# Last two blocks of a cross-attention kernel: seven-product queries and projections, and division behind the values

## Chip, cores and metric

One Trainium2 chip, one core. The metric is the device time of the whole kernel in microseconds, median of several runs. One further execution was profiled; its page, waits and timeline are what is read here.

## What is computed

x is 16 x 1024 x 512, the context 16 x 64 x 512, all float32. Both are layer-normalised with a scale and shift that depend on the condition, then 16 heads of width 32 attend from 1024 rows to 64 context rows.

```python
xq  = _ada_ln(x_q,  t_vec, Wss_q,  bss_q)
xkv = _ada_ln(x_kv, t_vec, Wss_kv, bss_kv)
q = (xq @ Wq + bq).reshape(B, Lq, nh, dh)
kv = (xkv @ Wkv + bkv).reshape(B, Lkv, 2, nh, dh)
k, v = kv[:, :, 0], kv[:, :, 1]
scores = jnp.einsum('bqhd,bkhd->bhqk', q, k) / jnp.sqrt(jnp.float32(dh))
attn = jax.nn.softmax(scores, axis=-1)
out = jnp.einsum('bhqk,bkhd->bqhd', attn, v).reshape(B, Lq, H)
return x_q + (out @ Wp + bp)
```

## The kernel before

The 16 x 1024 rows are cut into 32 blocks (0 to 31) of 512 rows; two blocks share a batch entry and its keys and values. The schedule is written out by hand: the calls stand in program order, every engine takes its own instructions in that order, and each waits only for the data and buffers that it needs. There is a way in (blocks 0 to 3), a loop over i = 4 to 29 (L1139 to L1233), and a way out (L1237 to L1293) in which y = 30 and z = 31. In the code below, `y - 1` is block 29 and `y - 2` block 28.

What happens to a block, and on which engine (PE is TensorE, DVE VectorE, ACT ScalarE, POOL GpSimd, SP the queue that issues DMAs):

- its rows are loaded, normalised (ACT), turned by DVE in squares of 32 and moved by 16 DMAs into a feature-major tile `xt`; `scale_features` (L562) applies scale and shift;
- queries: PE multiplies by Wq, a copy with bias goes to `qt`;
- `scores` (L666), in two halves z of the 64 context rows: PE fills two PSUM tiles of the pool `ps_s`; DVE reduces maxima out of each (L685) while ACT copies the scores to SBUF (L694). With `crossed` the two engines begin on different tiles;
- `maxima` (L721): the two halves' maxima are joined and spread out over a full tile (L716, 2.3 us on DVE); `subtract` (L727, two instructions), `weights` (L733, exponentials on ACT, two instructions);
- the sum of the weights, the product with the values (`mix`, L809, PE), division by the sum, projection by Wp, addition of x, and the write to DRAM.

Two forms exist for three of these steps.

**Queries.** The plain form (`queries`, L533) uses 16 matmuls of 512 columns. The form of the loop (`query_product`, L607) divides matrix and block into 2 x 2 parts and forms seven products instead of eight (four matmuls of 256 columns each), from sums of parts made beforehand on POOL (`query_weight_sums` once, `feature_sums` for each block, four instructions). The seven share two PSUM banks, `qa[0]` and `qa[1]`; `query_seed` copies one bank to the other, and four parts leave them by `query_out` (ACT, two instructions each) and `query_added` (DVE).

**Projection.** The plain form (`project` and `projected`, L849 to L868) makes four tiles of 128 rows, each in a bank of its own from a ring of four; one DVE addition to the residual and one write of 256 KB follow each. There the bias is added to the residual beforehand (`residual`, L330, on POOL). The form of the loop (`product`, `added`, L915 to L953) again has seven products, numbered 1 to 7, in two banks: `acc[2]` takes 1, 6, 5, 3 in that order, `acc[3]` takes 2, and, after a fresh filling, 7 and 4. `biased` (L891, ACT) fills a bank with the bias ahead of 1 and 7; `added` (DVE, L947) adds what the bank holds at that moment to a quarter of the residual, after every product. So a product that goes on in a bank has to wait until the addition of the one before has read it. `row_sums` (L903, POOL, two calls of two instructions) makes the sums of parts, partly in place.

**Division.** In the plain form DVE sums both halves of the weights (`sums`), inverts and spreads the result (`inverse`), and `divide` multiplies both weight tiles by it before `mix`. In the form of the loop POOL adds the two weight tiles (`total`, L765), DVE reduces the sum (`row_total`) and inverts it (`inverse_rows`), five DMAs take the small result to DRAM and back in another order, `spread_rows` (L792, DVE) spreads it, and `divided` (L800) multiplies the mixed values by it as they leave PSUM.

In the loop the two forms' waits are spread out: between `product(b, 6)` and `product(b, 5)` stand a query product of another block and half of the scores; between `product(a, 2)` and `product(a, 7)` stand four query products. The way out of the kernel before ends the loop form with block 28; blocks 29 to 31 take the plain projection, block 31 the plain queries, blocks 30 and 31 the plain division (block 29's is done behind the values). Block 31's scores use the buffers `big2` and `big3`, those of block 29. `load_residual` (L144) of block 30 takes the buffer of block 28's residual, so it waits for that block's last write; SP takes its DMAs in order behind it.

Of the kernel before, what the change touches and what calls it, by code (L numbers as in the profile page):

```python
# [9 lines left out]
F32 = mybir.dt.float32  # L10
# [10 lines left out]
def cross_attention_block(  # L21
# [88 lines left out]
    def bank(name, k=None):  # L110
        if k is None:
            k = ring.pop(0)
            ring.append(k)
        return ps_m.tile([P, TB], F32, tag=f"mm{k}", name=name)
# [215 lines left out]
    def residual(i, ts=range(NT)):  # L330
        for t in ts:
            nc.gpsimd.tensor_add(r_tiles[i][:, t, :], r_tiles[i][:, t, :], b_p_sb)
# [260 lines left out]
    def feature_sums(i):  # L593

        if "xt" not in sums_of:
            sums_of["xt"] = qpool.tile([P, 4, 2, HC, P], F32, tag="wq", name="xt_sums")
        t = sums_of["xt"]
        tt = nc.gpsimd.tensor_tensor
        b12 = feature_half(i, 0, 1)
        tt(t[:, 0], feature_half(i, 1, 1), b12, ALU.subtract)  # L600
        tt(b12, b12, feature_half(i, 0, 0), ALU.subtract)
        tt(t[:, 1], feature_half(i, 1, 1), b12, ALU.subtract)
        tt(t[:, 2], feature_half(i, 1, 0), t[:, 1], ALU.subtract)
# [62 lines left out]
    def scores(i, z, crossed=False):  # L666

        kt, qt = k_tiles[i // BPB], qt_tiles[i]
        pss = [ps_s.tile([P, 2, TB], F32, tag="s", name=f"ps_{i}_{z}_{e}") for e in range(2)]
        for r in range(HPC):  # L670
            rows = slice(32 * r, 32 * r + 32)
            for c in range(NC):
                nc.tensor.matmul(  # L673
                    pss[r // 2][32 * c : 32 * c + 32, r % 2, :],
                    lhsT=kt[rows, c, z * HK : (z + 1) * HK],
                    rhs=qt[rows, c, :],
                    start=True,
                    stop=True,
                )
        if z == 0:  # L680
            m_tiles[i] = small.tile([P, 2, HPC, NJ], F32, tag="m2", name=f"m2_{i}")
        s_sb = big.tile([P, HPC, TB], F32, tag=f"big{i % 2 * 2 + z}", name=f"s_{i}_{z}")

        def maximum(e):
            nc.vector.tensor_reduce(  # L685
                m_tiles[i][:, z, 2 * e : 2 * e + 2, :],
                pss[e].rearrange("p r (j a) -> p r j a", a=32),
                AX.X,
                ALU.max,
                apply_transpose=True,  # L690
            )

        def copied(e):
            nc.scalar.copy(s_sb[:, 2 * e : 2 * e + 2, :], pss[e])  # L694


        for step in (
            ((maximum, 0), (copied, 1), (maximum, 1), (copied, 0))
            if crossed
            else ((maximum, 0), (copied, 0), (maximum, 1), (copied, 1))  # L700
        ):
            step[0](step[1])
        s_tiles[i, z] = s_sb

    def both(dst, src, op):

        nc.vector.tensor_reduce(dst, src.rearrange("p z r j -> p (r j) z"), AX.X, op)

    def spread(i, src, name, other=False):
        if other:  # L710

            t = qpool.tile([P, 4, NC, NT * 32], F32, tag="xt", name=name)
            t = t.rearrange("p g c n -> p (g c n)")
        else:
            t = rpool.tile([P, HPC * TB], F32, tag="spread", name=name)
        nc.vector.transpose(t, src.unsqueeze(2).to_broadcast([P, HPC * NJ, 32]))  # L716
        return t.rearrange("p (r q) -> p r q", r=HPC)
# [3 lines left out]
    def maxima(i):  # L721

        m = small.tile([P, HPC * NJ], F32, tag="m", name=f"m_{i}")
        both(m, m_tiles.pop(i), ALU.max)
        mb_tiles[i] = spread(i, m, f"mb_{i}", other=i == NB - 1)

    def subtract(i, eng=nc.gpsimd, zs=(0, 1)):  # L727
        for z in zs:
            eng.tensor_tensor(s_tiles[i, z], s_tiles[i, z], mb_tiles[i], ALU.subtract)  # L729
# [3 lines left out]
    def weights(i, z):  # L733
        p = s_tiles[i, z]
        nc.scalar.activation(p, p, AF.Exp, scale=SCALE)  # L735
# [14 lines left out]
    def inverse(i):  # L750

        v = small.tile([P, HPC * NJ], F32, tag="v", name=f"v_{i}")
        both(v, l_tiles.pop(i), ALU.add)
        nc.vector.reciprocal(v, v)
        vb_tiles[i] = spread(i, v, f"vb_{i}", other=i in (1, NB - 1))

    def divide(i, eng=nc.gpsimd):
        vb = vb_tiles.pop(i)
        for z in range(2):
            eng.tensor_tensor(s_tiles[i, z], s_tiles[i, z], vb, ALU.mult)  # L760
# [3 lines left out]

    def total(i):  # L765

        t = big.tile([P, HPC, TB], F32, tag=f"big{(i + 1) % 2 * 2}", name=f"sum_{i}")
        nc.gpsimd.tensor_tensor(t, s_tiles[i, 0], s_tiles[i, 1], ALU.add)  # L768
        sum_tiles[i] = t

    def row_total(i):
        lt_tiles[i] = small.tile([P, HPC, NJ], F32, tag="lt", name=f"lt_{i}")
        nc.vector.tensor_reduce(
            lt_tiles[i],
            sum_tiles.pop(i).rearrange("p r (j a) -> p r j a", a=32),
            AX.X,
            ALU.add,
            apply_transpose=True,
        )

    def inverse_rows(i):

# [16 lines left out]

    def divided(i):  # L800
        vb = vb_tiles.pop(i)
        ot_tiles[i] = opool.tile([P, NC, TB], F32, tag="ot", name=f"ot_{i}")
        for e in range(2):
            cs = slice(2 * e, 2 * e + 2)
            nc.vector.tensor_tensor(ot_tiles[i][:, cs, :], po_tiles[i][e], vb[:, cs, :], ALU.mult)

    po_tiles, ot_tiles = {}, {}

    def mix(i, apart=True):  # L809

        vt = v_tiles[i // BPB]

        if apart:
            pairs = [ps_s.tile([P, 2, TB], F32, tag="s", name=f"po_{i}_{e}") for e in range(2)]
            po = [pairs[c // 2][:, c % 2, :] for c in range(NC)]
            po_tiles[i] = pairs
        else:
            po = [bank(f"po_{i}_{c}") for c in range(NC)]
            po_tiles[i] = po
        for z in range(2):  # L820
            p = s_tiles.pop((i, z))
            for c in range(NC):
                rows = slice(32 * c, 32 * c + 32)
                for r in range(HPC):
                    nc.tensor.matmul(  # L825
                        po[c][32 * r : 32 * r + 32, :],
                        lhsT=vt[rows, z, 32 * r : 32 * r + 32],
                        rhs=p[rows, r, :],
                        start=(z == 0),
                        stop=(z == 1),  # L830
                    )
# [110 lines left out]
    def added(i, n):  # L942

        m, o = {1: (0, 0), 2: (0, 0), 6: (0, 1), 7: (1, 1), 5: (1, 1), 4: (0, 1), 3: (1, 0)}[n]
        r = r_tiles[i][:, 2 * m : 2 * m + 2, o * HO : (o + 1) * HO]
        k = 2 if n in (1, 6, 5, 3) else 3
        nc.vector.tensor_add(r, acc[k].rearrange("p (t h) -> p t h", t=2), r)  # L947
        if n in (3, 4):
            nc.sync.dma_start(
                rows_of(out, i)[:, 2 * m : 2 * m + 2, :], r_tiles[i][:, 2 * m : 2 * m + 2, :]  # L950
            )
        if n == 3:
            r_tiles.pop(i)  # L953


    q_stats(0)
# [182 lines left out]
    for i in range(4, NB - 2):  # L1139
# [78 lines left out]
            q_stats(i + 4, (3,), kvb=kvb if kv == 0 else None)  # L1218
        query_product(n, 3)
        query_out(n, 3)  # L1220
        if f < NB - 1:
            feature_sums(f)
        else:
            residual(i)
        product(a, 7)
        row_total(i)
        inverse_rows(i)
# [7 lines left out]


    y, z = NB - 2, NB - 1  # L1237
    residual(z)
    scores(y, 0, crossed=True)
    product(y - 2, 6)  # L1240
    added(y - 2, 6)
    added(y - 2, 7)
    scores(y, 1)
    product(y - 2, 5)
    added(y - 2, 5)
    maxima(y)
    subtract(y, nc.vector)
    queries(z, 0)
    product(y - 2, 4)
    product(y - 2, 3)  # L1250
    spread_rows(y - 1)
    added(y - 2, 4)
    added(y - 2, 3)
    ring[:] = [1, 2, 3, 0]
    load_residual(y)
    mix(y - 1)
    divided(y - 1)
    weights(y, 0)
    queries(z, 1)
    sums(y, 0)  # L1260
    weights(y, 1)
    residual(y)
    queries(z, 2)
    sums(y, 1)
    queries(z, 3)
    inverse(y)
    divide(y)
    scores(z, 0)
    project(y - 1, 0)
    scores(z, 1)  # L1270
    maxima(z)
    project(y - 1, 1)
    subtract(z, nc.vector)
    project(y - 1, 2, later=True)
    mix(y)
    weights(z, 0)
    mixed(y, (0,))
    weights(z, 1)
    mixed(y, (1,))
    sums(z, 0)  # L1280
    projected(y - 1, 2)
    sums(z, 1)
    inverse(z)
    divide(z, nc.vector)
    project(y - 1, 3)
    project(y, 0)
    project(y, 1)
    project(y, 2)
    mix(z)
    mixed(z)  # L1290
    project(y, 3)
    for t in range(NT):
        project(z, t)  # L1293

# [1 line left out]
_INS = [  # L1296
# [37 lines left out]
```

## Time and profile before

| what | value |
|---|---|
| median of 3 runs | 1058.74 us |
| lowest, highest | 1057.19, 1059.29 us |
| profiled execution, time | 1058.86 us |
| profiled execution, span | 1057.1 us |
| busy in the span: PE | 1033.6 us (98%) |
| DVE, POOL, ACT | 854.7 (81%), 752.7 (71%), 618.0 us (58%) |
| one repetition of the loop (945.84 to 975.10) | 29.26 us |
| way out (975.10 to the end) | 82.0 us |

Times in the profile count from the start of the span; the execution's own time is 1.76 us longer than its span. A row of a timeline gives start, duration, engine, line, operation, what is written from what, and how many instructions were merged; in brackets stands how long the engine was idle before it and what ended that. PE's rows overlap slightly, since matmuls are pipelined.

### The profile page before, as it was taken

To read this page: it belongs to the slowest core of one execution; us is meant where nothing else is said; L and a number is where in the kernel's file an instruction comes from. 1 tells how busy PE (TensorE), PEld (TensorE's weight loads), DVE (VectorE), ACT (ScalarE), POOL (GpSimd) and SP (SyncE) were. 2 spreads that over 40 slices of the span, in tenths; PEclk is the share of its full clock that TensorE was granted. 3 is DMA by queue.
4 is the path that set the end of the run, shared out by engine and by line. 5 is a ranking of instruction groups with operands and counts; after the bars stand their busy time and mean duration, and the time that the engine had idled before them with its cause. 6 is when DMAs were issued, how large, how long until landed. Compare 5 with 4: busy or idle time off the path is not lost.

```text
span 1057.1 us, 22537 instructions
## 1 busy us (share of the span) xinstructions
PE 1033.6 (98%) x8914; PEld 733.7 (69%) x8914; DVE 854.7 (81%) x1134; ACT 618.0 (58%) x951; POOL 752.7 (71%) x470
## 2 busy tenths in 40 slices
PE   6999998999999999999999999999999999999998
PEld 4534365777777787777787787777777777777433
DVE  5698648987789877888878878898778887776993
ACT  3566665665575655667556666566566765565330
POOL 0258794889768869788668986688886886787340
PEclk9999999999999999999999999999999999999999
DMA  9743444444535344544345443444454443334202
GB/s 337 248 127 111 130 122 127 155 150 147 161 94 162 123 140 145 171 148 127 106 131 164 153 158 112 126 141 150 139 157 134 152 134 116 98 115 162 82 30 90
DMA packets 99976, 147.27 MB, mean 139 GB/s; under 512 B 29944, under 2 KB 30096, under 8 KB 99872
## 3 DMA queue, kind: packets, MB, share of 16 engines
q1 hardware_dynamic: 99872, 145.85, 43.5%
q8 instruction: 70, 1.15, 0.5%
q14 instruction: 34, 0.28, 0.1%
HBM read 78.85 MB, written 34.44 MB: 107 GB/s over the span
## 4 chain that ended last, share of the span: by engine, by line
PE 80%; DVE 5%; POOL 5%; DMA 4%; SPq 2%; issue 2%; ACT 1%; POOLq 0%; DVEq 0%; ACTq 0%
PE pp L933 28%; PE pq L625 27%; PE po L825 6%; PE ps L673 6%; PE pp L852 5%; PE pq L542 3%; SPq L508 2%; PE pv L431 2%; PE pk L395 2%; POOL s L760 2%; DMA wss_kv<-in_L_xcond_Wss_kv_dram 2%; DMA b_p_sb<-in_L_xcond_bp_dram 1%; POOL s L729 1%; DMA x<-in_x_dram 1%; DVE s L729 1%
## 5 line engine op out<-in xcount | busy, mean ns | idle before, releaser
L729 POOL TENSOR_TENSOR s<-s,mb 128x2048 f32<-128x2048 f32 x58 | 263.1, 4560 | 160.8 <-DVE mb L716 160.8
L694 ACT COPY s<-ps 128x1024 f32<-128x1024 f32 x128 | 129.5, 1012 | 119.7 <-DVE m L685 82.9
L685 DVE TRANSPOSE_TENSOR_REDUCE m<-ps 128x32 f32<-128x1024 f32 x128 | 150.6, 1214 | 27.1 <-PE ps L673 27.1
L655 ACT ACTIVATE qt<-pq,bias_t 128x256 f32<-128x256 f32 x208 | 85.8, 463 | 110.9 <-PE pq L625 110.9
L933 PE MATMUL pp<-w_p_sb,ot 128*128 128x256 f32 x648 | 148.7, 379 | 0.0
L735 ACT ACTIVATE s<-s 128x2048 f32<-128x2048 f32 x64 | 122.3, 1911 | 42.4 <-POOL s L729 31.8
L947 DVE TENSOR_TENSOR r<-pp,r 128x512 f32<-128x512 f32 x189 | 122.5, 670 | 25.5 <-PE pp L933 19.8
L933 PEld LDWEIGHTS pp<-w_p_sb,ot 128*128 128x128 f32 x648 | 123.4, 190 | 17.4 <-issue 0.7
L768 POOL TENSOR_TENSOR sum<-s,s 128x2048 f32<-128x2048 f32 x27 | 122.7, 4543 | 0.8 <-ACT s L735 0.8
L933 PEld LDWEIGHTS pp<-WT,s 128*128 128x128 f32 x432 | 78.9, 192 | 54.0 <-issue 29.3
L933 PE MATMUL pp<-WT,s 128*128 128x256 f32 x432 | 109.3, 397 | 0.0
L933 PE MATMUL pp<-WT,ot 128*128 128x256 f32 x432 | 102.2, 380 | 0.0
L625 PE MATMUL pq<-xt_sums,wq_sums 128*128 128x256 f32 x416 | 101.0, 386 | 0.0
L321 ACT ACTIVATE x<-x,rstdq 128x512 f32<-128x512 f32 x128 | 96.7, 807 | 4.8 <-POOL rstdq L285 3.2
L625 PE MATMUL pq<-xt,wq_sums 128*128 128x256 f32 x416 | 99.0, 381 | 0.0
L625 PEld LDWEIGHTS pq<-xt_sums,wq_sums 128*128 128x128 f32 x416 | 77.0, 190 | 31.1 <-issue 21.8
L625 PE MATMUL pq<-xt,w_q_sb 128*128 128x256 f32 x416 | 98.4, 380 | 0.1
L260 DVE BATCH_NORM_STATS2 bs<-x 128x6 f32<-128x512 f32 x128 | 86.9, 679 | 5.0 <-DMA x<-in_x_dram 5.0
L662 DVE TENSOR_TENSOR qt<-pq,qt 128x256 f32<-128x256 f32 x104 | 39.1, 418 | 63.1 <-PE pq L625 62.5
L933 PEld LDWEIGHTS pp<-WT,ot 128*128 128x128 f32 x432 | 82.2, 190 | 11.0
L565 ACT ACTIVATE xt<-xt,ss_q 128x512 f32<-128x512 f32 x112 | 84.7, 810 | 6.1 <-DMA xt<-ht 4.3
L625 PEld LDWEIGHTS pq<-xt,w_q_sb 128*128 128x128 f32 x416 | 79.1, 190 | 11.0 <-PE pp L933 0.4
(139 smaller groups left out, 1725.0 us busy)
## 6 DMA issues: line engine op xcount, KB each, us to landing
x<-in_x_dram SPq DMA_DIRECT2D x32, 1024.0 KB, 6.4
r<-in_x_dram SPq DMA_DIRECT2D x32, 1024.0 KB, 5.5
xt<-ht SPq DMA_DIRECT2D x496, 64.0 KB, 2.0
out_dram<-r SPq DMA_DIRECT2D x54, 512.0 KB, 3.8
out_dram<-r SPq DMA_DIRECT2D x20, 256.0 KB, 2.0
wss_q<-in_L_xcond_Wss_q_dram SPq DMA_DIRECT2D x2, 1024.0 KB, 8.8
ctx<-in_ctx_dram SPq DMA_DIRECT2D x8, 256.0 KB, 3.2
wss_kv<-in_L_xcond_Wss_kv_dram SPq DMA_DIRECT2D x2, 1024.0 KB
```

The lines of the kernel that those rows point to most:

```text
L260: nc.vector.bn_stats(bs, r)
L321: nc.scalar.activation(dst, src, AF.Identity, bias=rstd[:, 1, j : j + 1], scale=rstd[:, 0, j : j + 1])
L565: nc.scalar.activation(xt[:, :, c, :], xt[:, :, c, :], AF.Identity, scale=ss["q"][:, c, b : b + 1], bias=ss["q"][:, NC + c, b : b + 1],)
L625: nc.tensor.matmul(qa[k][:, m * HT : (m + 1) * HT].rearrange("p (g n) -> p g n", g=2), lhsT=a[:, c, m * P : (m + 1) * P], rhs=x[:, :, c, : ...
L655: nc.scalar.activation(dst, src, AF.Identity, bias=bq_t[:, o : o + 1])
L685: nc.vector.tensor_reduce(m_tiles[i][:, z, 2 * e : 2 * e + 2, :], pss[e].rearrange("p r (j a) -> p r j a", a=32), AX.X, ALU.max, apply_tra ...
L694: nc.scalar.copy(s_sb[:, 2 * e : 2 * e + 2, :], pss[e])
L729: eng.tensor_tensor(s_tiles[i, z], s_tiles[i, z], mb_tiles[i], ALU.subtract)
L735: nc.scalar.activation(p, p, AF.Exp, scale=SCALE)
L768: nc.gpsimd.tensor_tensor(t, s_tiles[i, 0], s_tiles[i, 1], ALU.add)
L933: nc.tensor.matmul(acc[k][:, t * HO : (t + 1) * HO], lhsT=rows[:, c, t * P : (t + 1) * P], rhs=cols[:, c, :], start=n == 2 and t == 0 and ...
L947: nc.vector.tensor_add(r, acc[k].rearrange("p (t h) -> p t h", t=2), r)
```

## The change

It keeps the loop but for its last repetition and rewrites the way out. Helpers get the variants that this needs: block 31's scores lie in `ht` and `xt`, block 30's total in `x`, block 30's divided values in `big2`, so that each has a place of its own; `mix` can be given its four banks; `divided` then goes bank by bank and fills `acc[2]` after the first; `halves_total` joins the two sums of block 31; the last block's `added` writes each finished quarter at once, the last one in two parts.

```diff
@@ -679,7 +679,12 @@
                 )
         if z == 0:
             m_tiles[i] = small.tile([P, 2, HPC, NJ], F32, tag="m2", name=f"m2_{i}")
-        s_sb = big.tile([P, HPC, TB], F32, tag=f"big{i % 2 * 2 + z}", name=f"s_{i}_{z}")
+        if i < NB - 1:
+            pool, tag = big, f"big{i % 2 * 2 + z}"
+        else:
+
+            pool, tag = ((hpool, "ht"), (qpool, "xt"))[z]
+        s_sb = pool.tile([P, HPC, TB], F32, tag=tag, name=f"s_{i}_{z}")
 
         def maximum(e):
             nc.vector.tensor_reduce(
@@ -722,7 +727,7 @@
 
         m = small.tile([P, HPC * NJ], F32, tag="m", name=f"m_{i}")
         both(m, m_tiles.pop(i), ALU.max)
-        mb_tiles[i] = spread(i, m, f"mb_{i}", other=i == NB - 1)
+        mb_tiles[i] = spread(i, m, f"mb_{i}", other=False)
 
     def subtract(i, eng=nc.gpsimd, zs=(0, 1)):
         for z in zs:
@@ -752,7 +757,7 @@
         v = small.tile([P, HPC * NJ], F32, tag="v", name=f"v_{i}")
         both(v, l_tiles.pop(i), ALU.add)
         nc.vector.reciprocal(v, v)
-        vb_tiles[i] = spread(i, v, f"vb_{i}", other=i in (1, NB - 1))
+        vb_tiles[i] = spread(i, v, f"vb_{i}", other=i == 1)
 
     def divide(i, eng=nc.gpsimd):
         vb = vb_tiles.pop(i)
@@ -764,7 +769,8 @@
 
     def total(i):
 
-        t = big.tile([P, HPC, TB], F32, tag=f"big{(i + 1) % 2 * 2}", name=f"sum_{i}")
+        pool, tag = (xpool, "x") if i == NB - 2 else (big, f"big{(i + 1) % 2 * 2}")
+        t = pool.tile([P, HPC, TB], F32, tag=tag, name=f"sum_{i}")
         nc.gpsimd.tensor_tensor(t, s_tiles[i, 0], s_tiles[i, 1], ALU.add)
         sum_tiles[i] = t
 
@@ -778,6 +784,10 @@
             apply_transpose=True,
         )
 
+    def halves_total(i):
+        lt_tiles[i] = small.tile([P, HPC, NJ], F32, tag="lt", name=f"lt_{i}")
+        both(lt_tiles[i].rearrange("p r j -> p (r j)"), l_tiles.pop(i), ALU.add)
+
     def inverse_rows(i):
 
         lt = lt_tiles.pop(i)
@@ -799,14 +809,22 @@
 
     def divided(i):
         vb = vb_tiles.pop(i)
-        ot_tiles[i] = opool.tile([P, NC, TB], F32, tag="ot", name=f"ot_{i}")
-        for e in range(2):
-            cs = slice(2 * e, 2 * e + 2)
-            nc.vector.tensor_tensor(ot_tiles[i][:, cs, :], po_tiles[i][e], vb[:, cs, :], ALU.mult)
+        pool, tag = (big, "big2") if i == NB - 2 else (opool, "ot")
+        ot = pool.tile([P, NC, TB], F32, tag=tag, name=f"ot_{i}")
+        ot_tiles[i] = ot
+        po = po_tiles.pop(i)
+        for e in range(len(po)):
+            if len(po) == NC:
+                nc.vector.tensor_tensor(ot[:, e, :], po[e], vb[:, e, :], ALU.mult)
+                if e == 0:
+                    biased(i, 2)
+            else:
+                cs = slice(2 * e, 2 * e + 2)
+                nc.vector.tensor_tensor(ot[:, cs, :], po[e], vb[:, cs, :], ALU.mult)
 
     po_tiles, ot_tiles = {}, {}
 
-    def mix(i, apart=True):
+    def mix(i, apart=True, ks=(None,) * NC):
 
         vt = v_tiles[i // BPB]
 
@@ -815,7 +833,7 @@
             po = [pairs[c // 2][:, c % 2, :] for c in range(NC)]
             po_tiles[i] = pairs
         else:
-            po = [bank(f"po_{i}_{c}") for c in range(NC)]
+            po = [bank(f"po_{i}_{c}", ks[c]) for c in range(NC)]
             po_tiles[i] = po
         for z in range(2):
             p = s_tiles.pop((i, z))
@@ -944,13 +962,21 @@
         m, o = {1: (0, 0), 2: (0, 0), 6: (0, 1), 7: (1, 1), 5: (1, 1), 4: (0, 1), 3: (1, 0)}[n]
         r = r_tiles[i][:, 2 * m : 2 * m + 2, o * HO : (o + 1) * HO]
         k = 2 if n in (1, 6, 5, 3) else 3
-        nc.vector.tensor_add(r, acc[k].rearrange("p (t h) -> p t h", t=2), r)
+        a = acc[k].rearrange("p (t h) -> p t h", t=2)
+        if i == NB - 1:
+
+            for ts in ((0,), (1,)) if n == 3 else ((0, 1),):
+                ts = slice(ts[0], ts[-1] + 1)
+                nc.vector.tensor_add(r[:, ts, :], a[:, ts, :], r[:, ts, :])
+                if n in (2, 3, 4, 5):
+                    dst = rows_of(out, i)[:, 2 * m : 2 * m + 2, o * HO : (o + 1) * HO]
+                    nc.sync.dma_start(dst[:, ts, :], r[:, ts, :])
+            return
+        nc.vector.tensor_add(r, a, r)
         if n in (3, 4):
             nc.sync.dma_start(
                 rows_of(out, i)[:, 2 * m : 2 * m + 2, :], r_tiles[i][:, 2 * m : 2 * m + 2, :]
             )
-        if n == 3:
-            r_tiles.pop(i)
 
 
     q_stats(0)
@@ -1218,10 +1244,7 @@
             q_stats(i + 4, (3,), kvb=kvb if kv == 0 else None)
         query_product(n, 3)
         query_out(n, 3)
-        if f < NB - 1:
-            feature_sums(f)
-        else:
-            residual(i)
+        feature_sums(f)
         product(a, 7)
         row_total(i)
         inverse_rows(i)
@@ -1235,62 +1258,112 @@
 
 
     y, z = NB - 2, NB - 1
-    residual(z)
     scores(y, 0, crossed=True)
     product(y - 2, 6)
     added(y - 2, 6)
+    query_product(z, 1)
+    query_seed(z)
     added(y - 2, 7)
     scores(y, 1)
     product(y - 2, 5)
     added(y - 2, 5)
     maxima(y)
-    subtract(y, nc.vector)
-    queries(z, 0)
+    subtract(y)
+    query_product(z, 2)
+    query_out(z, 2)
     product(y - 2, 4)
-    product(y - 2, 3)
     spread_rows(y - 1)
     added(y - 2, 4)
+    query_product(z, 6)
+    query_out(z, 6)
+    query_product(z, 7)
+    query_out(z, 7)
+    weights(y, 0)
+    query_product(z, 5)
+    query_added(z, 5)
+    query_product(z, 4)
+    query_added(z, 4)
+    query_product(z, 3)
+    query_out(z, 3)
+    weights(y, 1)
+    total(y)
+    product(y - 2, 3)
     added(y - 2, 3)
-    ring[:] = [1, 2, 3, 0]
     load_residual(y)
-    mix(y - 1)
+    scores(z, 0, crossed=True)
+    mix(y - 1, apart=False, ks=(2, 3, 1, 0))
     divided(y - 1)
-    weights(y, 0)
-    queries(z, 1)
-    sums(y, 0)
-    weights(y, 1)
-    residual(y)
-    queries(z, 2)
-    sums(y, 1)
-    queries(z, 3)
-    inverse(y)
-    divide(y)
-    scores(z, 0)
-    project(y - 1, 0)
+    row_sums(y - 1, 0)
+    row_total(y)
+    inverse_rows(y)
+    product(y - 1, 1)
+    added(y - 1, 1)
     scores(z, 1)
+    product(y - 1, 2)
+    added(y - 1, 2)
+    biased(y - 1, 3)
+    row_sums(y - 1, 1)
     maxima(z)
-    project(y - 1, 1)
-    subtract(z, nc.vector)
-    project(y - 1, 2, later=True)
+    product(y - 1, 7)
+    added(y - 1, 7)
+    subtract(z, nc.vector, (0,))
+    subtract(z, nc.gpsimd, (1,))
+    product(y - 1, 6)
+    added(y - 1, 6)
+    product(y - 1, 5)
+    added(y - 1, 5)
+    product(y - 1, 3)
+    added(y - 1, 3)
+    biased(y, 2)
+    weights(z, 0)
     mix(y)
-    weights(z, 0)
-    mixed(y, (0,))
+    spread_rows(y)
+    product(y - 1, 4)
+    divided(y)
+    row_sums(y, 0)
+    added(y - 1, 4)
     weights(z, 1)
-    mixed(y, (1,))
     sums(z, 0)
-    projected(y - 1, 2)
+    product(y, 1)
+    added(y, 1)
+    product(y, 2)
+    added(y, 2)
+    biased(y, 3)
+    row_sums(y, 1)
     sums(z, 1)
-    inverse(z)
-    divide(z, nc.vector)
-    project(y - 1, 3)
-    project(y, 0)
-    project(y, 1)
-    project(y, 2)
+    halves_total(z)
+    inverse_rows(z)
+    product(y, 7)
+    added(y, 7)
+    product(y, 6)
+    added(y, 6)
+    product(y, 5)
+    added(y, 5)
+    product(y, 3)
+    added(y, 3)
+    biased(z, 2)
     mix(z)
-    mixed(z)
-    project(y, 3)
-    for t in range(NT):
-        project(z, t)
+    spread_rows(z)
+    product(y, 4)
+    divided(z)
+    row_sums(z, 0)
+    added(y, 4)
+    product(z, 1)
+    added(z, 1)
+    product(z, 2)
+    added(z, 2)
+    biased(z, 3)
+    row_sums(z, 1)
+    product(z, 7)
+    added(z, 7)
+    product(z, 6)
+    added(z, 6)
+    product(z, 5)
+    added(z, 5)
+    product(z, 4)
+    added(z, 4)
+    product(z, 3)
+    added(z, 3)
```

## The prediction

> **What bounds the kernel now.** I compared the last repetition of the loop with the way out by stages, then read TensorE's timeline of the way out, then those of the engines that its new waits would be for. First the stages; after the stage come each engine's busy time and count, then TensorE's clock.
>
> ```profile
> 945.84:975.10 29.26, 29.26 (x242) 22.42 (x241) 20.48 (x23) 15.49 (x21) 23.73 (x12) 1.00 0.46 147
> 975.10:1005.00 29.90, 29.40 (x229) 14.52 (x229) 29.62 (x25) 10.71 (x11) 12.70 (x11) 1.00 0.21 73
> 1005.00:1035.00 30.00, 28.17 (x198) 10.84 (x211) 28.23 (x19) 9.37 (x8) 12.07 (x5) 1.00 0.07 27
> 1035.00:1057.10 22.10, 18.32 (x72) 7.58 (x44) 5.06 (x8) 1.93 (x2) 0.00 (x0) 0.97 0.28 107
> ```
>
> In the loop TensorE (PE) never rests and VectorE (DVE) has 30% free. In the way out PE still hardly rests, but DVE is as full: 29.6 of 29.9 us and 28.2 of 30.0. So there are two near bounds there, and it matters who waits for whom. PE's own rows, from the timeline:
>
> ```profile
> 971.55 1.89 PE L625 MATMUL pq<-xt,wq_sums 128*128 128x256 f32 x8
> 973.28 1.89 PE L933 MATMUL pp<-WT,ot 128*128 128x256 f32 x8
> 975.10 1.14 PE L673 MATMUL ps<-qt,kt 32*32 32x512 f32 x32
> 976.17 2.00 PE L933 MATMUL pp<-WT,s 128*128 128x256 f32 x8
> ...
> 1003.32 3.70 PE L852 MATMUL pp<-w_p_sb,ot 128*128 128x512 f32 x8
> 1006.95 1.14 PE L673 MATMUL ps<-qt,kt 32*32 32x512 f32 x32
> ...
> 1033.61 2.35 PE L825 MATMUL po<-s,vt 32*32 32x512 f32 x64
> 1035.88 17.43 PE L852 MATMUL pp<-w_p_sb,ot 128*128 128x512 f32 x40
> ```
>
> Rows overlap by the pipeline's tail, so I take start to start: one of the seven products 1.73 us (971.55 to 973.28), a half of the scores 1.07, the values 2.28, a whole projection tile 3.44. The way out starts at 975.10 with block 30's scores; PE ends at about 1053.3.
>
> The rows that follow PE, and the one wait that I expect to be new:
>
> ```profile
> L685 DVE TRANSPOSE_TENSOR_REDUCE m<-ps 128x32 f32<-128x1024 f32 x128 | 150.6, 1214 | 27.1 <-PE ps L673 27.1
> L947 DVE TENSOR_TENSOR r<-pp,r 128x512 f32<-128x512 f32 x189 | 122.5, 670 | 25.5 <-PE pp L933 19.8
> ...
> 968.31 0.83 ACT L655 ACTIVATE qt<-pq,bias_t 128x256 f32<-128x256 f32 x2
> 969.02 0.60 ACT L896 COPY pp<-b_diff 128x512 f32<-128x512 f32 x1
> ...
> 1008.07 8.99 POOL L760 TENSOR_TENSOR s<-s,vb 128x2048 f32<-128x2048 f32 x2
> ...
> 1013.70 7.72 DVE L729 TENSOR_TENSOR s<-s,mb 128x2048 f32<-128x2048 f32 x2
> ...
> L729 DVE TENSOR_TENSOR s<-s,mb x6: 2278/2288/5518, 54.0 to 1019.1; 128x2048 f32<-128x2048 f32 x6
> ```
>
> An addition costs 0.65, a bias copy 0.6, a maximum 1.2. Of the six DVE subtractions five take about 2.29 us and one 5.52: it began at 1013.70, while GpSimd (POOL) multiplied until 1017.06, and ended at 1019.22, 2.16 after POOL.
>
> **What the Trainium skill says.** "SBUF — State Buffer", section "SBUF: two separate sides": a VectorE operation with two SBUF inputs and a GpSimd operation that reads SBUF take a shared port pair as an exclusive lock; whoever starts second stands for the other's whole instruction. The 5.52 us agrees. "Trainium Kernel Development and Optimization", section "Key Constraints": GpSimd cannot reach PSUM, so the seven products' additions stay on DVE, as all of L947 are. "TensorE: Matmul & The Clock Gate", section "Part 1: The HAM clock gate": an idle window of about 3.4 us halves TensorE's clock, a busy one restores it. Here the granted clock fell at about 1055.9, 2.6 us after the last matmul; and after 3.57 us of idle at 10.92 the 32 matmuls of L231 took 1.93 us, against 1.08 for the same number at 14.88.
>
> **What is taken from PE.** Work from 975.10: 32 products (block 28's last 4, 7 query products of 31, 7 each for blocks 29, 30, 31) at 1.73 are 55.4; four halves of scores 4.3; three mixes 6.8; about nine changes between shapes at 0.1 are 0.9: 67.4 us. Now it takes 78.2. The gain at stake is **10.8 us**, if the new order waits nowhere.
>
> **What that form makes PE wait for.** Products share two accumulating banks. After product 6 its sum is read (starts 0.2 after PE, takes 0.65) before 5 may add onto the same bank: 0.9 us. Likewise 5 before 3. After product 2 come its addition and then a bias copy before 7: 0.2 + 0.65 + 0.1 + 0.6 + 0.05 = 1.6. In the loop query products stand between; at the end they are spent. Bare turnarounds: 1.6 three times, 0.9 five times: 9.3 us. The rest is DVE's queue, which I wrote out operation by operation:
>
> Up to 996.5 PE has no wait: query product 1 fills the 0.5 us it waited before block 30's second scores. Maxima of 30 end a little later, the broadcast at 986.55. POOL subtracts to 995.75 (2 x 4.53), exponentials end at 997.7, POOL's total at 1002.3. Block 31's scores run 996.5 to 997.6, the mix of 29 to 999.85. DVE finishes 31's maxima at 1000.1, then divides the first quarter (0.65); with the bias copy PE starts product 1 at 1001.5: **1.65 idle**.
>
> DVE goes on: division to 1002.6, row total of 30 (2.3) and reciprocal (0.57) to 1005.5, addition 1 to 1006.15, 31's other maxima to 1008.5, addition 2 to 1009.15; ScalarE (ACT) copies scores until 1009.6 and the bias until 1010.2. PE ran out of products at 1006.2, product 7 starts at 1010.25: **4.05 idle**.
>
> The broadcast of 31's maxima ends at 1011.75. POOL starts its half of the subtraction at 1011.85 and holds the port to 1016.4. DVE must first add product 7 (PE ends 1012.0, addition at 1012.85); its half then stands until 1016.4 and ends at 1018.6. Queued behind it is addition 6, at 1019.25, for which product 5 waits; PE ended 6 at 1013.75: **5.55 idle**. Then 0.9 before 3, which ends at 1023.7.
>
> Mix of 30 to 1026.0, product 4 of 29 to 1027.75. The reciprocals' broadcast (2.3) and the first division give product 1 of 30 at 1028.1: 0.4 idle with product 2's 0.05. DVE then has addition 4, sums of 31 (2.3), additions 1 and 2 to 1033.4, the bias copy to 1034.1; PE has been out since 1031.65: **2.5 idle**. Twice 0.9 follows; mix of 31 at 1042.95 to 1045.25, product 4 of 30 to 1047.0. Block 31: 0.4 before 1 and 2, 1.6 before 7, 0.9 before 5; product 4 covers addition 5. Total idle 1.65 + 4.05 + 5.55 + 0.9 + 0.4 + 2.5 + 1.8 + 0.4 + 2.5 = **19.75 us**. PE ends at 975.1 + 67.4 + 19.75 = 1062.2.
>
> **What costs nothing, and its cover.** Feature sums (4 x 1.27 on POOL) replace additions of the bias there, end at 981.2 and are needed at 985.9; later than that each us is one for PE. Query outputs (8 x 0.41 on ACT) and two pairs of additions (0.76 each) lie beside the next query product; without that they would cost 0.9 each. The seed copy (0.57) lies beside scores. Own places for 31's scores and 30's total: the old readers are done, so no wait. Row sums (1.27 each) lie beside products 1 and 2; the third is done by 1006.2, before product 6 asks for it. The reciprocals' round trip issues five DMAs on SP behind the residual load of 30, which waits for 28's last write (about 1001); from reciprocal to landing 5.3 us (976.5 to about 981.7 now), so 1010.8 and 1041.9, needed at 1024.5 and 1043.8. If a landing slips by over 1.9 us, the last mix's division slips. Removed from the path: 31's division on DVE (4.5) and 30's on POOL (9.0), which PE waited for 0.9 us in all.
>
> **The end.** Last addition in halves is not shown at this place: 0.38 to 0.42 by L662 (same 256 columns); I take 0.4. A last write of half the size: landing between the 1.5 us of a 32 KB transfer and the 2.0 of 256 KB, plus 1 us to the span's end, so 2.5 to 3.05; I take 3.0. 1062.2 + 0.2 + 0.4 + 3.0 = 1065.8, against the span of 1057.1: +8.7. The profiled execution took 1058.86, median 1058.74; the difference carries over, **1067.4 us**. Division in quarters, also not shown, is between 0.59 (half of L805's 1.17) and 0.69 (L947's shape); four are +-0.2. The reduction of two halves is as L707's, 0.29.
>
> **Rivals.**
> No lock (0.14): subtraction 31 takes 2.3 beside POOL, addition 6 is ready at 1015.8, product 5 starts 3.4 earlier: 1064.0. Against it stands the 5.52 us.
> Clock lost (0.11): with 4.05 and 5.55 idle, longer than the 2.6 after which the clock fell, matmuls slow by 1.93/1.08. After the first gap that is hidden behind the lock; after the second, products 5 and 3 pay up to 1.4 each, about 2.4: 1069.8.
> Turnarounds only (0.07): DVE's queue has slack that I do not see, 9.3 idle remain: 1057.0, no difference.
> PE covered as in the loop (0.15), the other side: the same calls at 945.84 to 975.10 leave PE no idle at all. If additions stay as well hidden here, idle is the 2.3 us of now: 67.4 + 2.3 ends PE at 1044.8, 1050.0. It decides once total idle is under 10.9 us. Against it: no other product stands between 6 and 5.
>
> **Numbers.** My forecast has 0.53. Its unknowns (a dozen waits at +-0.15 each, the end, the quarters) make it 1065.0 to 1069.5. The range takes in no lock, most of lost clock and turnarounds only: 1057.0 to 1070.5; 0.15 lie below, little above. Slower by over 0.2% (what a measurement can tell from no change) is 0.53 + 0.14 + 0.11 = 0.78, same 0.07, faster 0.15.
>
> **What would show it.** Right: PE idle of about 4 us before product 7 of 29 and 5 before its 5, released by ACT's copy and DVE's addition; a DVE subtraction of about 5.7 us that ends 2.2 after POOL's. Wrong: total PE idle after 975 under 11 us, or DVE idle where PE waits.

## The result, and the profile after

The change makes the kernel **slower by about 1.1%**: 1070.14 us (four runs, 1069.2 to 1070.92) against 1059.01 (four runs, 1057.19 to 1060.44), ratio 1.0114, interval 1.0102 to 1.0127. The forecast had the direction and most of the size (+8.7 us, 1067.4). Its range ended at 1070.5: the median lies inside, but the ratio times the old median, 1058.74 x 1.0114 = 1070.8, lies above. So the range was too low at its upper end.

The profiled execution has a span of 1069.1 us (before: 1057.1). Its way out runs from 974.61 to the end, 94.5 us instead of 82.0. By stages, the columns as before:

```profile
945.84:975.10 29.26, 29.26 (x263) 22.30 (x240) 20.43 (x23) 15.49 (x21) 23.72 (x12) 1.00 0.47 147
975.10:1005.00 29.90, 28.43 (x293) 20.71 (x262) 22.42 (x27) 14.31 (x18) 22.40 (x11) 1.00 0.23 73
1005.00:1035.00 30.00, 18.11 (x126) 12.74 (x124) 23.49 (x19) 7.33 (x7) 11.42 (x7) 0.94 0.11 38
1035.00:1069.10 34.10, 26.33 (x160) 19.55 (x160) 15.07 (x19) 1.18 (x2) 5.04 (x4) 0.95 0.18 64
```

In the third line PE is busy for 18.1 of 30 us (before: 28.2), and DVE has become less busy too, 23.5. The two now wait for each other in turn. TensorE's granted clock in the last two lines is 0.94 and 0.95; before it was 1.00 and, with the time behind the last matmul in it, 0.97. PE's timeline, with the idle time ahead of a row and what ended it:

```profile
1001.03 1.99 PE L951 MATMUL pp<-w_p_sb,ot 128*128 128x256 f32 x8 [1.47 <-ACT pp L914]
...
1009.46 1.97 PE L951 MATMUL pp<-WT,ot 128*128 128x256 f32 x8 [3.44 <-ACT pp L914]
1011.27 1.89 PE L951 MATMUL pp<-WT,s 128*128 128x256 f32 x8
1018.35 3.44 PE L951 MATMUL pp<-WT,s 128*128 128x256 f32 x8 [5.19 <-DVE r L975]
1022.58 1.99 PE L951 MATMUL pp<-WT,ot 128*128 128x256 f32 x8 [0.79 <-DVE r L975]
...
1034.93 3.65 PE L951 MATMUL pp<-WT,ot 128*128 128x256 f32 x8 [2.25 <-ACT pp L914]
1038.42 1.89 PE L951 MATMUL pp<-WT,s 128*128 128x256 f32 x8
1041.09 1.99 PE L951 MATMUL pp<-WT,s 128*128 128x256 f32 x8 [0.78 <-DVE r L975]
...
1055.50 1.97 PE L951 MATMUL pp<-WT,ot 128*128 128x256 f32 x8 [1.50 <-POOL ot L931]
```

Every wait of the forecast is there, in its order, and all but one with its releaser: product 7 of block 31 was let go by POOL's row sums, which ended at 1055.44, 0.08 us after the bias copy. The reader is to look at the second column as well: eight matmul records of one product take 1.9 to 2.0 us, but 3.44 at 1018.35 and 3.65 at 1034.93. The lock, on DVE and POOL:

```profile
1011.54 0.69 DVE L975 TENSOR_TENSOR r<-pp,r 128x512 f32<-128x512 f32 x1 [0.64 <-PE pp L951]
1012.14 5.55 DVE L734 TENSOR_TENSOR s<-s,mb 128x2048 f32<-128x2048 f32 x1
1017.62 0.68 DVE L975 TENSOR_TENSOR r<-pp,r 128x512 f32<-128x512 f32 x1
```

```profile
1011.04 4.51 POOL L734 TENSOR_TENSOR s<-s,mb 128x2048 f32<-128x2048 f32 x1 [3.61 <-DVE mb L721]
```

POOL ends at 1015.55, DVE's subtraction at 1017.69, 2.14 later (before: 2.16), and only then comes the addition that product 5 waits for. The chain of waits goes the same way: through DVE's subtraction to its addition, and from there to PE.

```profile
1012.14 1.09 DVE s L734
1013.23 4.39 issue
1017.62 0.69 DVE r L975
1018.30 0.04 issue
1018.35 3.46 PE pp L951 x8
```

And the clock in those stretches (the number after POOL's):

```profile
1016.00:1018.00 2.00, 0.00 (x0) 0.00 (x0) 2.00 (x2) 0.00 (x0) 0.00 (x0) 0.98 0.00 0
1018.00:1020.00 2.00, 1.65 (x4) 1.38 (x5) 0.29 (x1) 0.00 (x0) 0.00 (x0) 0.50 0.00 0
...
1035.00:1037.00 2.00, 2.00 (x5) 1.64 (x6) 1.93 (x3) 0.00 (x0) 0.00 (x0) 0.50 0.00 0
```

It is halved twice, at about the moment when a wait ends (1017.9 and 1035.0). So the theory to be tested: the loss is PE waiting for its shared banks behind a locked and full DVE, and the clock adds to the longer waits. Rivals: DVE's sheer amount of work is the bound, or the slow products have another cause.

### The profile page after: what moved, and what is told of

The parts are those of the page before. It is cut to its first block, busy times and chain, and to the rows that moved or that the text cites. A ratio compares the mean times of both kernels' runs of the same rounds, so it can differ in the third digit from the quotient of the medians.

```text
span 1069.1 us, 22787 instructions
## 1 busy us (share of the span) xinstructions
PE 1030.4 (96%) x9010; PEld 752.3 (70%) x9010; DVE 852.8 (80%) x1147; ACT 618.4 (58%) x958; POOL 767.8 (72%) x476
## 3 DMA queue, kind: packets, MB, share of 16 engines
q8 instruction: 71, 1.16, 0.5%
## 4 chain that ended last, share of the span: by engine, by line
PE 85%; DVE 5%; DMA 4%; POOL 2%; SPq 2%; issue 1%; ACT 0%; POOLq 0%; DVEq 0%
PE pp L951 34%; PE pq L625 31%; PE po L843 6%; PE ps L673 6%; PE pq L542 2%; PE pv L431 2%; PE pk L395 2%; PE pp L870 2%; POOL s L765 2%; DMA wss_kv<-in_L_xcond_Wss_kv_dram 1%; SPq L508 1%; DMA b_p_sb<-in_L_xcond_bp_dram 1%; DMA x<-in_x_dram 1%; DVE l L745 1%; DVE m L690 1%
## 5 line engine op out<-in xcount | busy, mean ns | idle before, releaser
L734 POOL TENSOR_TENSOR s<-s,mb 128x2048 f32<-128x2048 f32 x61 | 276.7, 4561 | 166.9 <-DVE mb L721 166.9
L951 PE MATMUL pp<-w_p_sb,ot 128*128 128x256 f32 x720 | 165.9, 380 | 1.9 <-ACT pp L914 1.5
L975 DVE TENSOR_TENSOR r<-pp,r 128x512 f32<-128x512 f32 x203 | 132.1, 671 | 39.7 <-PE pp L951 33.3
L951 PEld LDWEIGHTS pp<-w_p_sb,ot 128*128 128x128 f32 x720 | 136.3, 190 | 24.9 <-issue 4.0
L951 PEld LDWEIGHTS pp<-WT,s 128*128 128x128 f32 x480 | 87.7, 192 | 63.2 <-issue 31.9
L774 POOL TENSOR_TENSOR sum<-s,s 128x2048 f32<-128x2048 f32 x28 | 127.1, 4540 | 2.7 <-ACT s L740 2.7
L951 PE MATMUL pp<-WT,s 128*128 128x256 f32 x480 | 120.8, 395 | 6.8 <-DVE r L975 6.0
L951 PE MATMUL pp<-WT,ot 128*128 128x256 f32 x480 | 115.6, 384 | 8.7 <-ACT pp L914 5.7
L951 PEld LDWEIGHTS pp<-WT,ot 128*128 128x128 f32 x480 | 91.8, 192 | 23.2 <-POOL ot L931 4.5
L625 PEld LDWEIGHTS pq<-xt,wq_sums 128*128 128x128 f32 x432 | 80.7, 190 | 11.4 <-issue 1.2
```

Of the source, the lines that this page charges most:

```text
L625: nc.tensor.matmul(qa[k][:, m * HT : (m + 1) * HT].rearrange("p (g n) -> p g n", g=2), lhsT=a[:, c, m * P : (m + 1) * P], rhs=x[:, :, c, : ...
L951: nc.tensor.matmul(acc[k][:, t * HO : (t + 1) * HO], lhsT=rows[:, c, t * P : (t + 1) * P], rhs=cols[:, c, :], start=n == 2 and t == 0 and ...
L975: nc.vector.tensor_add(r, a, r)
```

## The experiments

The start of the way out differs by some us between executions (972.8 to 977.4) with equal code before it. So beside the times I give the length of the way out in each profile, from block 30's first scores to the end: before 82.0, after 94.5.

**1. Subtraction on POOL alone.**

```diff
-    subtract(z, nc.vector, (0,))
+    subtract(z, nc.gpsimd, (0,))
```

> Both halves of block 31's subtraction on POOL, one after the other, so that DVE never asks for the port. Theory of the port lock: DVE is free for addition 6 of block 29 at once, product 5 follows 6 after about 0.9 us instead of 5.2, and its matmuls keep the full clock (1.73 us instead of 3.46); mix of 30 starts about 6 us earlier and the time falls to about 1064. The exponentials of 31 come later (POOL ends the second half about 1020) and are covered. Rival, that DVE is simply full there and the lock is incidental: only DVE's own 2.3 us go, 1067 to 1068.

Measured: 1066.23 us, ratio to before 1.0093 (1.0064 to 1.0122), in two groups: 1063.27 and 1063.54, 1069.33 and 1068.93. The profiled execution is of the shorter pair, way out 87.3:

```profile
1009.02 1.96 PE L951 MATMUL pp<-WT,ot 128*128 128x256 f32 x8 [3.44 <-ACT pp L914]
1010.82 1.89 PE L951 MATMUL pp<-WT,s 128*128 128x256 f32 x8
1013.49 1.99 PE L951 MATMUL pp<-WT,s 128*128 128x256 f32 x8 [0.78 <-DVE r L975]
...
1028.62 1.97 PE L951 MATMUL pp<-WT,ot 128*128 128x256 f32 x8 [2.25 <-ACT pp L914]
```

The 5.19 us became 0.78, as the lock's theory says, and neither product 7 is slow. In that execution the way out is 7.2 us shorter. The wait gives 4.4 of them, and the two products at full clock 1.4 and 1.7 (start to the next start, block 29's product 5 and block 30's product 7); 0.35 are lost again in a longer wait for block 31's division. The other two runs, 5.7 us longer, weren't profiled, but the mean granted clock of every run is on record: 0.998 in the shorter pair, 0.994 in the longer. So the clock was lower there; in which waits it fell isn't shown.

**2. Subtraction on DVE, but later.** 
```diff
     added(y - 1, 7)
-    subtract(z, nc.vector, (0,))
     subtract(z, nc.gpsimd, (1,))
...
     biased(y, 2)
+    subtract(z, nc.vector, (0,))
     weights(z, 0)
```

> The subtraction stays on DVE but in the program after addition 3 of block 29, when POOL has ended its half. Theory of the queue (what costs is that the additions stand behind the blocked subtraction): DVE takes 2.29 us for it, product 5 waits 0.9 us at full clock, but the spread and the division of block 30 stand 2.3 us later: about 1066. Rival, that the long DVE operation costs the same wherever it stands: no change from 1070.

Measured: 1069.36 us, ratio 1.0108 (1.009 to 1.0126), way out 93.0. The DVE subtraction takes 2.28 us without POOL beside it, and product 5 waits 0.78. The gain was nevertheless given back, at other places:

```profile
1009.65 3.75 PE L951 MATMUL pp<-WT,ot 128*128 128x256 f32 x8 [3.44 <-ACT pp L914]
1013.20 3.02 PE L951 MATMUL pp<-WT,s 128*128 128x256 f32 x8
...
1028.39 5.38 PE L951 MATMUL pp<-w_p_sb,ot 128*128 128x256 f32 x16 [2.42 <-DVE ot L823]
```

The clock fell in the wait of 3.44 us, which had left it alone in the first experiment, and again in a new wait of 2.42 for block 30's division, which stands behind the moved subtraction. After the first, product 7 takes 3.55 us to the next start and product 6 2.8 (1.8 and 1.73 after the change); after the second, two products' records take 5.38 us instead of 3.69. One of the four runs took 1066.29, close to what I expected, at a mean clock of 0.997; the others, 1069.17 and more, had 0.991 to 0.995.

**3. The gaps filled.** `fill` issues matmuls of 256 columns on constant weights into bank 0, which nobody reads.

```diff
     product(y - 1, 2)
+    fill("fill_0", 6)
...
     product(y - 1, 6)
+    fill("fill_1", 10)
...
     product(y, 2)
+    fill("fill_2", 4)
```

> Matmuls that nobody reads fill PE's three long waits in part: 6 (2.6 us) before product 7 of block 29, 10 (4.3 us) before its product 5, 4 (1.7 us) before product 7 of block 30. No wait gets shorter. Theory of the clock: PE does not rest long enough to lose it, product 5 of 29 and product 7 of 30 take 1.73 us instead of 3.46, and the time falls by 3.4 us, to about 1066.7. Rival, that these two products were slow for another reason (operands just written, the restart of PE): no change or up to 1 us slower.

Measured: 1066.3 us, ratio 1.0085 (1.007 to 1.01), way out 91.4, 3.1 less than after.

```profile
1012.45 4.48 PE L1263 MATMUL fill<-w_q_sb 128*128 128x256 f32 x20
1017.82 1.99 PE L951 MATMUL pp<-WT,s 128*128 128x256 f32 x8 [0.89 <-DVE r L975]
...
1030.55 1.89 PE L1263 MATMUL fill<-w_q_sb 128*128 128x256 f32 x8
1032.96 1.97 PE L951 MATMUL pp<-WT,ot 128*128 128x256 f32 x8 [0.52 <-ACT pp L914]
```

DVE's releases come as before, but the products behind them run in 2.0 us. Useless work makes the kernel 3 to 4 us faster: that the clock costs this is shown.

**4. A bank of its own for products 7 and 4.** Its bias is copied in early; the copy between 2 and 7 is gone. For block 29 (30 and 31 likewise):

```diff
     divided(y - 1)
+    biased_apart(y - 1, 1)
     row_sums(y - 1, 0)
...
     added(y - 1, 2)
-    biased(y - 1, 3)
```

> Products 7 and 4 of blocks 29 to 31 get a PSUM bank of their own, whose bias is copied in before product 1, so that 7 need not wait for addition 2 and the copy. Theory of shared banks and a full DVE queue: in block 29 nothing is won, since product 5 still stands behind the locked subtraction; in block 30 the waits move from 7 to 5 (DVE is at the sums of 31), about 2.5 us won, the clock's 1.7 with them or not; in block 31 the 1.5 us go. Together 1070 falls by 4 to 6, to about 1065. Rival, that the waits at 7 are what sets the end in each block: 3.4 + 2.3 + 1.5 + 1.7 go, 1061.

Measured: 1069.25 us, ratio 1.0113 (1.0096 to 1.0129): nothing won in time; by the profile the way out is 92.1, 2.4 shorter. The waits at 7 are gone in all three blocks. In blocks 29 and 30 they come back at 5; block 31's 1.5 us are won:

```profile
1010.33 1.89 PE L958 MATMUL pp<-WT,s 128*128 128x256 f32 x8
1021.08 3.78 PE L958 MATMUL pp<-WT,s 128*128 128x256 f32 x8 [8.86 <-DVE r L984]
...
1041.56 3.54 PE L958 MATMUL pp<-WT,s 128*128 128x256 f32 x8 [2.35 <-DVE r L984]
```

One wait removed from a queue that DVE sets is handed on to the next product; both still cost the clock. The rival that these waits set the end by themselves falls.

**5. Experiment 1 with two of the fillings** (before product 7 of blocks 29 and 30).

```diff
+    fill("fill_0", 6)
...
-    subtract(z, nc.vector, (0,))
+    subtract(z, nc.gpsimd, (0,))
...
+    fill("fill_2", 4)
```

> Both halves of 31's subtraction on POOL, as in the first experiment, and 6 and 4 unread matmuls in PE's waits before product 7 of blocks 29 and 30. If the clock made that experiment's executions fall into two groups (1063.3 and 1069.1), this one has one group near the lower, 1063 to 1064, and its two products 7 take 1.73 us; if something else split them, it is split again.

Measured: 1064.35 us, all four between 1063.26 and 1064.94, ratio 1.0053 (1.0032 to 1.0075), way out 87.3. One group, near the lower, with a mean clock of 0.998 in every run: with experiment 1's 0.998 and 0.994 this points to the clock as what split it.

**6. One part alone: seven-product queries in the kernel before.** `queries(z, 0)` to `queries(z, 3)` are replaced by the seven products at their places; the feature sums come ahead of two residual additions on POOL. The last two replacements:

```diff
-    queries(z, 2)
+    query_product(z, 5)
+    query_added(z, 5)
+    query_product(z, 4)
+    query_added(z, 4)
     sums(y, 1)
-    queries(z, 3)
+    query_product(z, 3)
+    query_out(z, 3)
```

> The kernel before with one part of the change: block 31's queries from seven products (feature sums at the end of the loop, the bias of 29's and 31's residuals after them), all else as before. Theory that a seven-product form gains where other work stands between its products: 28 short matmuls for 16 long ones take 1.7 us from PE and fill the 0.5 us wait before the second scores of 30, so 1056 to 1057, against 1058. Rival, that these waits too show up in PE: 1059 or more.

Measured: 1061.47 us (20 runs) against 1058.11, ratio 1.003 (1.0022 to 1.0039). The profiled execution is the shortest of the twenty (1058.86), way out 84.3. Here too the form with less work loses:

```profile
993.22 1.89 PE L625 MATMUL pq<-xt_sums,w_q_sb 128*128 128x256 f32 x8
999.29 3.60 PE L625 MATMUL pq<-xt,wq_sums 128*128 128x256 f32 x8 [4.18 <-DVE qt L662]
```

```profile
996.31 2.29 DVE L740 TRANSPOSE_TENSOR_REDUCE l<-s 128x64 f32<-128x2048 f32 x1
998.53 1.37 DVE L662 TENSOR_TENSOR qt<-pq,qt 128x256 f32<-128x256 f32 x4
```

I had put the queries' additions behind a sum of weights on DVE (2.29 us, after 2.3 of division). In the changed kernel the same products run without any wait from 985.68 to 994.3, since DVE has nothing ahead of their additions there. My expectation missed this.

**7. Plain projections.** Queries and division as changed, but blocks 29 to 31 with a bank for each tile; both halves of the subtraction on POOL; block 31's second scores right after the mix of 29, its maxima after the row total of 30; bias in the residual.

```diff
     mix(y - 1, apart=False, ks=(2, 3, 1, 0))
+    scores(z, 1, later=True)
     divided(y - 1)
...
+    project(y - 1, 0)
+    project(y - 1, 1)
     weights(z, 0)
     mix(y)
     spread_rows(y)
     divided(y)
```

> The changed kernel's queries and its division behind the values, but the plain projection for blocks 29 to 31 (a bank for each tile, the bias in the residual), both halves of 31's subtraction on POOL, 31's second scores straight after the mix of 29. Theory that the shared banks are the loss: PE does 5 us more than in the changed kernel, 72.4 in all, and nearly never waits, so the end is near 1053. Rival, that DVE is the bound of the way out in any form: PE idle 8 us or more remains, 1060 or above.

Measured: **1053.84 us** (eight runs), ratio 0.996 (0.9948 to 0.9972), way out 77.0. PE does more and waits less:

```profile
1007.28 2.57 PE L851 MATMUL po<-s,vt 32*32 32x512 f32 x64
1009.78 17.43 PE L878 MATMUL pp<-w_p_sb,ot 128*128 128x512 f32 x40
1027.14 2.35 PE L851 MATMUL po<-s,vt 32*32 32x512 f32 x64
1029.42 17.43 PE L878 MATMUL pp<-w_p_sb,ot 128*128 128x512 f32 x40
```

Between 1000 and the end no wait of PE is listed. DVE as the bound in any form is refuted. This run changes banks, order and subtraction together; experiment 11 parts them.

**8 and 9. Seven products for blocks 30 and 31, with cover.** Plain projection for 29; own bank for 7 and 4; order 1, 2, 7, 6, 4, 5, 3. In the first version both row sums stood ahead of product 2, which therefore read rows already altered by them: it computes something else for product 2, and waited for POOL (4.95 and 3.20 us). The end of block 30 against experiment 7:

```diff
-    project(y, 0)
-    project(y, 1)
-    project(y, 2)
+    product(y, 4)
+    added(y, 4)
+    biased_apart(z, 1)
+    product(y, 5)
+    added(y, 5)
     mix(z)
     spread_rows(z)
+    product(y, 3)
     divided(z)
```

> As the plain-projection kernel, but blocks 30 and 31 from seven products again, with a bank of its own for 7 and 4, and in the order 1, 2, 7, 6, 4, 5, 3, with the mix of 31 between 5 and 3 of block 30. Theory: with a product of another bank behind each sum PE does not wait for additions, so the 3.4 us less of PE work are won but for 1 to 3 us of waits at the start of block 31: 1051 to 1053. Rival: DVE, which has 14 additions instead of 8 there, is late for each: 1055 or more.

Measured: 1065.39 us, way out 88.3. With the second row sums behind product 2:

```diff
-    row_sums(y, 1)
...
     product(y, 2)
+    row_sums(y, 1)
```

> The kernel with seven products for blocks 30 and 31 (own bank for 7 and 4, order 1, 2, 7, 6, 4, 5, 3), with the second row sums after product 2 in the program, so that 2 reads the rows before they are altered and no longer waits for POOL. Theory: the waits of 4.95 and 3.20 us before product 2 of the run before go, one of about 1 us before product 7 of block 30 and one of 1 us before block 31 stay: 1052 to 1054, level with plain projections or 1 us below. Rival, that POOL, busy with 31's subtraction until 1020, is late for 30's row sums in any order: 1056 or more.

Measured: **1052.73 us**, ratio 0.9946 (0.9931 to 0.9961), way out 76.3. Two waits over half a us are left, 0.68 before product 7 of 30 and 0.79 before product 3 of 31.

**10. Seven products for block 31 alone**, otherwise as experiment 7.

```diff
     divided(z)
+    row_sums(z, 0)
+    biased(z, 2)
+    biased_apart(z, 1)
     project(y, 3)
-    for t in range(NT):
-        project(z, t)
+    product(z, 1)
+    added(z, 1)
+    product(z, 2)
+    row_sums(z, 1)
```

> The plain-projection kernel with seven products for block 31 alone, where POOL has nothing else to do. Theory: 1.7 us of PE work less, 0.9 us for the addition before product 3, the last write smaller: 0.5 to 1 us below plain projections, 1053 to 1053.5. Rival, that the row sums and the copies at the start of block 31 make PE wait: 1055 or more.

Measured: **1052.35 us**, ratio 0.994 (0.9925 to 0.9955), way out 76.0. Both versions beat the two kernels of the case; which of 9 and 10 is better these runs don't tell.

**11. The change with plain projections only**, its order and its shared subtraction kept.

```diff
-    product(y - 1, 7)
-    added(y - 1, 7)
+    project(y - 1, 1)
     subtract(z, nc.vector, (0,))
     subtract(z, nc.gpsimd, (1,))
-    product(y - 1, 6)
-    added(y - 1, 6)
+    project(y - 1, 2)
```

> The change with one part undone: blocks 29 to 31 get plain projections in four banks, while the order of the other steps stays as in the change, the subtraction shared by DVE and POOL with it. Theory: no product waits for an addition any more (waits at 7, 5 and 3 gone), but DVE is still held up to 1019 and then comes to the division of 30 only at 1025, so that one wait of about 5 us is left ahead of block 30's projection: about 1060. Rival, that the shared banks are the whole loss: 1054, as with plain projections and the subtraction on POOL.

Measured: 1064.99 us, ratio 1.0057 (1.0041 to 1.0074), way out 89.7; I expected 1060.

```profile
1021.68 12.19 PE L868 MATMUL pp<-w_p_sb,ot 128*128 128x512 f32 x24 [3.70 <-DVE ot L821]
...
1042.99 16.91 PE L868 MATMUL pp<-w_p_sb,ot 128*128 128x512 f32 x32 [3.21 <-DVE ot L821]
```

The wait for 30's division is there (3.70). I had missed the second: 31's sums stand behind two additions on DVE and end late, the reciprocals' way through DRAM ends at 1038.9, and the last division is late by 3.2. Both waits cost the clock as well: 24 matmul records take 12.1 us by their starts instead of 10.3, 32 take 16.9 instead of about 14. So the shared banks are not the whole loss: against the kernel before, plain projections alone bring the loss from 1.1% to 0.6%, about 6 us, and experiment 7, with the subtraction on POOL and another order on top, a further 1% or 10 us. These two weren't tried one by one.

## Why the prediction was right and where it was wrong

**PE's work: nearly right.** It was 68.2 us, as what remains of the 90.7 from 974.6 to PE's end when the waits and the slowed products below are taken off; forecast 67.4.

**The waits: right, each within 0.5 us.** Taken start to start, before product 1, 7, 5, 3 of block 29: 1.55, 3.6, 5.35, 0.77 (forecast 1.65, 4.05, 5.55, 0.9); block 30: 0.38, 2.4, 0.94, 0.95 (0.4, 2.5, 0.9, 0.9); block 31: 0.42, 1.68, 0.94 (0.4, 1.6, 0.9). Sum 19.0 against 19.75. That this 0.75 and the 0.8 of work cancel is luck.

**The lock: right.** 5.55 us for the subtraction, 2.14 after POOL; in experiment 2 the operation takes 2.28 us without POOL beside it, and in experiments 1 and 2 product 5 waits 0.78. This agrees with the Trainium skill, "SBUF — State Buffer", section "SBUF: two separate sides". It works the other way too: in experiment 11 four POOL additions that began behind DVE's blocked subtraction took 7.03 us instead of the 4.96 of the four before.

**The end: right.** From the last addition to the span's end 2.9 us, forecast 3.0.

**The clock: the term that failed.** The sum had 0 for it, and the rival "Clock lost" said that after the first gap it is hidden and that "after the second, products 5 and 3 pay up to 1.4 each", with a chance of 0.11. What the runs showed in its place: product 5 of block 29 took 3.46 us instead of 1.73, product 3 paid nothing, and product 7 of block 30 paid too, 3.49 to the next start instead of 1.81, after a wait of only 2.25 to 2.4 us that I had not counted as long enough although the profile of before showed the clock fall after 2.6. Together 3.4 us: 974.6 + 68.2 + 19.0 + 3.4 = 1065.2, and PE ended at 1065.3. Since the wait behind the slow product 5 came out shorter, the clock cost **3.1 us** net: 4.23 us from product 5's start to product 3's, against 2.78 in block 30, and 1.68 at product 7. Experiment 3 took the same 3.1 us off the way out by keeping the clock alone. The factor was too low as well: I used 1.93/1.08 = 1.8, measured is 2.0. The pair of rows that I took it from shows no lowered clock: the trace of before reads 1.00 there. With the term at its size the forecast is 1067.4 + 3.1 = 1070.5, against the 1070.8 of the ratio.

**The rival on the other side** ("PE covered as in the loop", 1050.0) was wrong for this order, but its condition fits what came later: in experiments 9 and 10 a product of another bank or a mix stands behind all but the last sums, PE hardly waits, and the time is 1052 to 1053 us. These runs moved the subtraction to POOL as well.

**Which waits of 2 to 3.5 us lose the clock.** "TensorE: Matmul & The Clock Gate", section "Part 1: The HAM clock gate", says that the activity window runs freely. The traces agree: in the way out of each the clock changes only at moments that lie 3.41 us, or a multiple of it, apart. Cut at these moments, the profile after gives (PE's busy time first, the clock behind POOL's):

```profile
1004.25:1007.67 3.42, 1.77 (x8) 1.22 (x7) 3.39 (x5) 0.99 (x1) 2.62 (x3) 1.00 0.14 38
1007.67:1011.08 3.41, 1.62 (x8) 1.47 (x9) 3.19 (x4) 1.53 (x3) 0.04 (x1) 1.00 0.08 7
1014.49:1017.91 3.42, 0.00 (x0) 0.00 (x0) 3.42 (x2) 0.00 (x0) 1.06 (x1) 1.00 0.00 0
1017.91:1021.32 3.41, 2.97 (x7) 2.43 (x8) 0.38 (x1) 0.00 (x0) 0.00 (x0) 0.50 0.00 0
1031.56:1034.97 3.41, 1.16 (x7) 0.71 (x5) 3.31 (x4) 0.59 (x1) 2.49 (x2) 1.00 0.38 150
1034.97:1038.39 3.42, 3.42 (x8) 2.76 (x9) 2.25 (x3) 0.00 (x0) 0.00 (x0) 0.50 0.04 9
```

A boundary parts the wait of 3.44 us into two stretches that both keep over 1.6 us of work, and the clock stays; the wait of 2.25 lies within one stretch, which keeps 1.16, and the clock is halved for the next. In the way outs of all the traces, up to the last matmul, the eleven stretches ahead of a loss had at most 1.17 us of work, and those at full clock that kept it at least 1.62; the half clock ended only behind a stretch with 2.97 or more and stayed on behind 2.48 or less. So the same wait can cost or not by where it falls: before product 7 of block 29 it left 1.77 and 1.62 after the change, but 0.99 in one stretch in experiment 2. Two things stay open: no run moved a wait against the stretches by itself, and busy time is not the whole measure, since near 75.8 us of the same trace, with other matmuls, a stretch with 2.46 us of work lost the clock. Nor did a run take back the division behind the values alone.

## What to carry to other kernels

A form with fewer products is worth its saving only while its dependent steps have other work between them. Count the turnarounds through the engine that empties the bank, and put that engine's whole queue into the sum: here a saving of 10.8 us, 2.3 of them old waits, met 19 us of waiting. A wait of TensorE of over some 2 us should be priced with a possibly lost clock: on this kernel 1.4 to 1.8 us where TensorE worked through one stretch of 3.41 us at half clock, and about 3 where two did (experiments 2 and 11). Where the cover runs out, at the end of a kernel, separate banks and more work can be faster than shared banks and less.

## What was not expected of the hardware

In the way out the clock was lost after waits as short as 2.25 us (after), 2.35 (experiment 4) and 2.42 (experiment 2), and kept after 3.44 (after, experiment 1) and 2.25 (experiment 1); all waits of 3.7 us or more lost it, none of 1.5 or less did. Once lost it was halved for 3.41 us, or for 6.83 (experiments 2, 8 and 11) and 10.24 (experiment 4), and never for a time between.
